# Graph attention's scores as two more columns of the values' product, row vectors turned on VectorE, queries and keys in one tile

## The chip, the cores and the metric

The kernel runs on one core of a Trainium2 chip. The metric is the device time of one execution in microseconds. The core has five engines that run their own instruction streams in order and meet through semaphores: TensorE (PE, matrix products and transposes, which write to the accumulation memory PSUM), VectorE (DVE), ScalarE (ACT), GpSimd (POOL) and SyncE (SP), whose queue issues nearly all of this kernel's DMA transfers.

## The reference

Four graph layers over eight independent batches of 2048 nodes with 128 features, all float32, on one 0/1 adjacency matrix. Before each layer stands a layer norm and a ReLU, and each layer's result is added to its input:

```python
h = maximum(layernorm(x), 0); x = x + layer0(h, adj, W, a, node_weights, ...)
h = maximum(layernorm(x), 0); x = x + layer1(h, adj, W_q, W_k, W_v, W_o, b_o)
h = maximum(layernorm(x), 0); x = x + layer2(h, adj, W_self, W_neigh, ...)
h = maximum(layernorm(x), 0); x = x + layer3(h, adj, W, a)
```

Layers 0 and 3 are graph attention. Their scores come from two dot products of each node's projected features h (layer 0's h is normalised once more, scaled by gamma and shifted by beta):

```python
s1 = h @ a[:128]; s2 = h @ a[128:]                  # two numbers for each node
e = leaky_relu(s1[:, :, None] + s2[:, None, :], 0.2)
att = softmax(where(adj > 0, e, -inf)); out = att @ h
```

Layer 1 is masked attention with four heads of 32. Layer 2 is a mean over the neighbours and two products. Layer 0 ends in an ELU, layer 2 in a ReLU.

## The kernel before, in words

One batch is four chunks g of 512 nodes, each a tile of 128 partitions x 4 x 128 features; nodes are also counted in 16 tiles of 128. At the start, mask_steps reads the adjacency (16 x 1 MB) and writes packed and transposed masks to DRAM, while layer0_ahead(0) prepares the first batch.

The backbone is layer 1's attention, all heads and batches: mains is a list of small steps (12 for each block of 256 rows and one head), which use PE for scores (L876), transposes (L912) and values (L927), DVE for the masked scores with their minimum (L892), and ACT for the exponentials (L900) and the copies of the transposed weights (L917). All other layers are side work. Function work puts the side steps between the main steps so that the weights given by hand are used up evenly over the batch. While batch b is in layer 1, the side does layers 2 and 3 of batch b - 1 and layer 0 of batch b + 1. For the first batch and for layers 2 and 3 of the last there is nothing to put them beside.

The order of instructions on PE, DVE, ACT and POOL is the order in which the code calls them (manual_schedule); the waits between engines are put in by the framework. SP's DMAs follow their places in the code.

A product in PSUM is read late. psum takes one of three buffers of two banks each from pool ps2, and later puts off the reader until the next side step begins (settle) or until buffers run short; the attention holds up to three of them itself.

What the change touches:

- layer0_ahead runs over the chunks in a skewed pipeline of stages: load, first layer norm, weigh (POOL), turned (PE transposes, ACT copy), project (rows_times with w0, ACT copy to haug, L561), second layer norm, scale and shift (POOL, L567 and L570), turned2 (PE transposes of haug, ACT copy h0nT), gat_scores.
- gat_scores (L374) multiplies each transposed tile on PE with the two vectors a (tile psc, L383); DVE copies the columns to s1 and s2 and makes s2n (L386 to L388). Layer 3 does the same with h3T and the vectors W a (wa3).
- along_free (L355) makes a row that all partitions hold from a column over partitions: PE transposes it to PSUM (prow, L360), DVE copies it (row, L364), SP writes it to DRAM (rowd, L366), and a second DMA broadcasts it to all partitions (L367). gat_rows does this with s2n for tile s2b, once for a layer. spread does it for each of the six groups of rows in gat_loop, with s1 and the row maximum in tile cab, for tile ab.
- gat_loop's groups: gat_maximum (L404) takes the maximum of s2 over the neighbours, shifts makes cab, spread sends it, then leaky (ACT, L464), lowered (DVE, L470), exps (ACT, L474), masked (DVE, L479) and product (PE, L490) run over the columns. A group's rows are sent while the group before is in its loop; a layer's first group has only its own ahead steps before it.
- before_attention.project makes queries (pq, L643) and keys (pk, L652) in two PSUM tiles, each with an ACT copy (qs, kc) and a DMA to DRAM.

Of the kernel before, what the change touches and what calls it, by code (L numbers as in the profile page):

```python
# [31 lines left out]
def gnn_kernel(  # L32
# [104 lines left out]
    def chunk(s):  # L137

        return new(cp, "c", s, (P, 512))
# [36 lines left out]
    nc.gpsimd.memset(neg_half, -0.5)  # L176

# [10 lines left out]
    w0 = load_w("w0", W0)  # L188
# [16 lines left out]
    NR = 2 * T + 4  # L205
# [4 lines left out]
    nc.scalar.dma_start(out=rows[2 * T + 2 : NR], in_=a3.rearrange("(c f) o -> c (f o)", c=2))  # L210
# [76 lines left out]
    def norm_stages(src, dst, relu=False):  # L287
# [44 lines left out]

        return [stats, root, shift, apply_relu] if relu else [stats, root, apply]
# [14 lines left out]
    def rows_times(srcT, w, name):  # L348

        pt = psum(name)  # L350
        for k in range(4):
            nc.tensor.matmul(pt[:, k, :], srcT[:, k * P : (k + 1) * P], w, start=True, stop=True)
        return pt

    def along_free(col, dst):  # L355


        n = col.shape[1]
        pt = psum("prow", (n, P))
        nc.tensor.transpose(pt, col, ident)  # L360

        def read():
            row = small("row", (T, P))[0:n, :]
            nc.vector.tensor_copy(row, pt)  # L364
            d = new(dr2, "rowd", "rowd", (T, P))
            nc.sync.dma_start(out=d[0:n, :], in_=row)  # L366
            nc.sync.dma_start(  # L367
                out=dst, in_=d[0:n, :].rearrange("t p -> (t p)").partition_broadcast(P)
            )

        later(read)


    def gat_scores(st, g, hT, a12):  # L374

        if g == 0:
            st["s1"] = small("s1", (P, T))
            st["s2"] = small("s2", (P, T))
            st["s2n"] = small("s2n", (P, T))
        c = slice(4 * g, 4 * g + 4)  # L380
        pc = psum("psc", (P, 4, 2))
        for k in range(4):
            nc.tensor.matmul(pc[:, k, :], hT[:, k * P : (k + 1) * P], a12, start=True, stop=True)  # L383

        def read():
            nc.vector.tensor_copy(st["s1"][:, c], pc[:, :, 0])  # L386
            nc.vector.tensor_copy(st["s2"][:, c], pc[:, :, 1])
# [20 lines left out]
    def gat_loop(st, finish, maxima):  # L408
# [20 lines left out]
        def shifts(k):  # L429
# [4 lines left out]
            cab = small("cab", (P, 6))[:, 0 : 2 * n]  # L434
# [101 lines left out]
    def layer0_ahead(b):  # L536

        st, h, hT, h2T = {}, {}, {}, {}
# [17 lines left out]
        def project(g):  # L556
# [4 lines left out]
            later(lambda: nc.scalar.copy(st["haug"][:, 4 * g : 4 * g + 4, 0:P], pt))  # L561
# [10 lines left out]
        def turned2(g):  # L572
            h2T[g] = chunk("h0nT")
            turn(hv(g), h2T[g])
# [7 lines left out]
            + norm_stages(hv, hv)  # L582
            + [scale, shift, turned2, lambda g: gat_scores(st, g, h2T.pop(g), a12_0)],
# [37 lines left out]
    def before_attention(b):  # L621
# [19 lines left out]
        def project(g):  # L641
            pq = psum("pq", (P, 512))
            nc.tensor.matmul(pq, wq, hT[g], start=True, stop=True)  # L643

            def read_q():
                qs = chunk("qs")
                nc.scalar.activation(qs, pq, AF.Copy, scale=-1.0 / (math.sqrt(HD) * UP))
# [4 lines left out]
            nc.tensor.matmul(pk, wk, hT[g], start=True, stop=True)  # L652

            def read_k():
# [650 lines left out]
```

## Time and profile before

| | |
|---|---|
| median of 3 runs | 4863.75 us (4861.99 to 4867.91) |
| the profiled execution | 4871.3 us, span 4869.5 us |
| PE, DVE, ACT busy | 4236.4, 3863.5, 3643.9 us |
| a steady batch (891 to 1462 us) | 571.0 us |
| granted PE clock, mean | 0.946 |
| DMA | 423.37 MB, mean 87 GB/s |

In the profile a group is a line of the kernel with one shape: how often it ran, its busy time, the mean of one, and the idle time of its engine just before it, with what ended that. PEld is PE's load of weights. The chain of waits follows the execution back from its last instruction, at each step to what released it. A stretch is a piece of the span with the busy time of each engine in it.

### The profile page before, as it was taken

To read this page: it belongs to the slowest core of one execution; us is meant where nothing else is said; L and a number is where in the kernel's file an instruction comes from. 1 tells how busy PE (TensorE), PEld (TensorE's weight loads), DVE (VectorE), ACT (ScalarE), POOL (GpSimd) and SP (SyncE) were. 2 spreads that over 40 slices of the span, in tenths; PEclk is the share of its full clock that TensorE was granted. 3 is DMA by queue.
4 is the path that set the end of the run, shared out by engine and by line. 5 is a ranking of instruction groups with operands and counts; after the bars stand their busy time and mean duration, and the time that the engine had idled before them with its cause. 6 is when DMAs were issued, how large, how long until landed. Compare 5 with 4: busy or idle time off the path is not lost.

```text
span 4869.5 us, 88275 instructions
## 1 busy us (share of the span) xinstructions
PE 4236.4 (87%) x34037; PEld 2898.0 (60%) x34037; DVE 3863.5 (79%) x8268; ACT 3643.9 (75%) x5153; POOL 437.4 (9%) x407
## 2 busy tenths in 40 slices
PE   3668998898998889898898988988899988999976
PEld 3545655565656666475665656566565656656645
DVE  5957776788978888788987889788887888758849
ACT  4637986697858888497885978588884888848926
POOL 2020002001200021001200012000210000000000
PEclk7868999999999999999999999999999999999988
DMA  8421123213231132312333132421324113222122
GB/s 269 135 88 54 47 61 97 92 49 102 81 126 57 57 107 79 124 50 76 91 105 95 57 94 85 122 65 55 107 76 130 48 58 98 79 86 62 47 92 75
DMA packets 303741, 423.37 MB, mean 87 GB/s; under 512 B 55844, under 2 KB 173016, under 8 KB 299224
## 3 DMA queue, kind: packets, MB, share of 16 engines
q1 hardware_dynamic: 301376, 416.84, 28.2%
q8 instruction: 269, 4.41, 0.4%
q14 instruction: 152, 1.25, 0.1%
q10 hardware_dynamic: 1944, 0.87, 0.1%
HBM read 365.77 MB, written 55.98 MB: 87 GB/s over the span
## 4 chain that ended last, share of the span: by engine, by line
PE 40%; DVE 31%; ACT 21%; issue 4%; DMA 4%; SPq 0%; POOL 0%; ACTq 0%; DVEq 0%; POOLq 0%
DVE e L892 9%; PE gacc L490 9%; PE pt L912 9%; ACT eT L917 6%; ACT e L900 6%; PE pagg L737 6%; PE sc L876 5%; DVE dump L404 5%; DVE ge L479 4%; DVE ge L470 4%; PE acc L927 4%; ACT ge L464 4%; ACT ge L474 2%; DVE ln_s L297 1%; DMA ab<-rowd 1%
## 5 line engine op out<-in xcount | busy, mean ns | idle before, releaser
L917 ACT COPY eT<-pt 128x1024 f32<-128x1024 f32 x1024 | 1018.4, 1011 | 666.4 <-PE pt L912 663.2
L892 DVE CUSTOM_DVE_ANT_0 e<-sc,pm 128x1024 f32<-128x1024 f32 x1024 | 1211.3, 1220 | 214.7 <-PE sc L876 205.6
L912 PE MATMUL pt<-ident,e 128*128 128x128 f32 x8192 | 1098.5, 282 | 187.0 <-DVE amh L892 106.0
L490 PE MATMUL gacc<-haug,ge 128*128 128x129 f32 x8192 | 1114.1, 286 | 123.4 <-DVE ge L479 121.2
L490 PEld LDWEIGHTS gacc<-haug,ge 128*128 128x128 f32 x8192 | 1011.9, 198 | 264.4 <-issue 134.7
L912 PEld LDWEIGHTS pt<-ident,e 128*128 128x128 f32 x8192 | 940.2, 145 | 341.4 <-DVE amh L892 137.4
L900 ACT ACTIVATE e<-e,amn 128x2048 f32<-128x2048 f32 x512 | 1027.8, 2007 | 20.9 <-DVE amn L896 20.8
L464 ACT ACTIVATE ge<-ab,s 128x384 f32<-128x384 f32 (+1 forms) x1536 | 800.6, 574 | 96.6 <-DMA ab<-rowd 96.3
L876 PE MATMUL sc<-ks,qr 32*128 32x512 f32 x4096 | 765.2, 668 | 55.8 <-ACT eT L917 40.5
L470 DVE TENSOR_TENSOR ge<-ge,ab 128x768 f32<-128x768 f32 (+1 forms) x768 | 666.4, 869 | 112.5 <-ACT ge L464 107.6
L479 DVE SCALAR_TENSOR_TENSOR ge<-mg,ge 128x768 f32<-128x768 fp8e4 (+1 forms) x768 | 662.0, 863 | 87.3 <-ACT ge L474 85.2
L474 ACT ACTIVATE ge<-ge 128x768 f32<-128x768 f32 (+1 forms) x768 | 591.5, 772 | 78.4 <-DVE ge L470 75.0
L927 PE MATMUL acc<-eT,vv 128*32 128x256 f32 x8192 | 612.5, 400 | 3.9 <-ACT eT L917 3.8
L404 DVE CUSTOM_DVE_ANT_0 dump<-s2b,pmg 128x2048 bf16<-128x2048 f32 x256 | 584.7, 2284 | 28.4 <-DMA s2b<-rowd 23.8
L307 POOL TENSOR_TENSOR ln_r<-ln_ve,neg_half 128x4 f32<-128x4 f32 x160 | 224.9, 1405 | 3872.8 <-DVE ln_ve L301 3781.0
L927 PEld LDWEIGHTS acc<-eT,vv 128*32 128x32 f32 x8192 | 196.6, 111 | 509.1 <-issue 430.2
L876 PEld LDWEIGHTS sc<-ks,qr 32*128 32x128 f32 x4096 | 231.9, 190 | 230.7 <-ACT eT L917 120.5
L737 PE MATMUL pagg<-mt,hm 128*128 128x512 fp8e4 x1536 | 356.7, 381 | 7.9 <-DVE agT L755 7.9
L737 PEld LDWEIGHTS <-hm 128*128 128x128 bf16 x1536 | 147.2, 98 | 182.0 <-issue 30.2
L339 PE MATMUL ptr<-ident,h 128*128 128x128 f32 x512 | 93.1, 308 | 46.1 <-DVE h L314 16.6
L980 DVE TENSOR_TENSOR aoT<-po,rT 128x256 f32<-128x256 f32 x64 | 27.1, 424 | 125.0 <-ACT rT L975 125.0
L339 PEld LDWEIGHTS ptr<-ident,h 128*128 128x128 f32 x512 | 65.5, 154 | 87.2 <-issue 26.6
(120 smaller groups left out, 2779.4 us busy)
## 6 DMA issues: line engine op xcount, KB each, us to landing
pmg<-pm_all SPq DMA_DIRECT2D x256, 256.0 KB
mg<-mg_all SPq DMA_DIRECT2D x128, 384.0 KB
pm<-pm_all SPq DMA_DIRECT2D x128, 256.0 KB
qr<-qd SPq DMA_DIRECT2D x1024, 32.0 KB
mt<-mt_all SPq DMA_DIRECT2D x64, 512.0 KB
ab<-rowd SPq DMA_DIRECT2D x64, 384.0 KB
adj<-in_adj_dram SPq DMA_DIRECT2D x16, 1024.0 KB
s2b<-rowd SPq DMA_DIRECT2D x16, 1024.0 KB
```

Of the source, the lines that this page charges most:

```text
L404: nc.vector.tensor_tensor_reduce(dump, st["s2b"], pm, UP, HIGHEST, ALU.add, ALU.min, st["mn"][:, it : it + 1])
L464: nc.scalar.activation(e[:, c, :], gr[k]["s1"], AF.Prelu, bias=st["s2"][:, j : j + 1], alpha=ALPHA)
L470: nc.vector.tensor_tensor(e, e, bc_mid(gr[k]["m"], 2), ALU.subtract)
L479: nc.vector.scalar_tensor_tensor(e, mt, BIG, e, ALU.mult, ALU.min)
L490: nc.tensor.matmul(gr[k]["acc"][:, q, :], e[:, c, q * P : (q + 1) * P], st["haug"][:, j, :], start=(j == 0 and q == 0), stop=(j == T - 1), ...
L737: nc.tensor.matmul(st["pa"], st["hm"][:, j, s, :], st["mt", g, j // 8][:, j % 8, :], start=(j == 0 and s == 0), stop=(j == T - 1 and s == ...
L876: nc.tensor.matmul(blk["sc"][g // 2][:, (g % 2) * 512 : (g % 2 + 1) * 512], blk["q"][r, t * P : (t + 1) * P], ks_t[b, hh][r, :], start=Tru ...
L892: nc.vector.tensor_tensor_reduce(e[:, c], blk["sc"][h], pm[:, c], UP, HIGHEST, ALU.add, ALU.min, mh[:, h : h + 1])
L900: nc.scalar.activation(blk["e"][t], blk["e"][t], AF.Exp, scale=-1.0, bias=blk["mn"][:, t : t + 1], accum_out=blk["ao"]["sum"][:, t, blk["h ...
L912: nc.tensor.transpose(pt[:, c, t, :], blk["e"][t][:, j * P : (j + 1) * P], ident)
L917: nc.scalar.copy(eT, blk.pop(("pt", w)).rearrange("p c t n -> p c (t n)"))
L927: nc.tensor.matmul(pair["acc"][g * HD : (g + 1) * HD, blk["hh"] % 2, :], vv_t[blk["b"], blk["hh"]][:, j, :], blk["eT"][w][:, g, :], start= ...
```

## The change

The scores of both graph attention layers become two more columns of the product that makes the values. For layer 3, W a is appended to W's transpose (w3T becomes 128 x 130). For layer 0, W (gamma a) is appended to w0; since the norm lies between, DVE corrects the two columns with the mean, the inverse root and two pairs of constants (gab: the sums of gamma a and of beta a). The transposes turned2 and the products psc go. The stage gat_scores of layer 0 stands before the norm is applied, and in layer 3 it is part of the reading of the product.

along_free turns a 128 x 32 tile on DVE in blocks of 32 x 32, and four DMAs, one for each 32 partitions, write the pieces to DRAM; its reading is no longer put off. The tiles cab and s2n become fixed tiles of 32 columns. Queries and keys share one PSUM tile, and both are read after both products. The set-up computes the additional columns.

```diff
--- before.py
+++ after.py
@@ -174,6 +174,15 @@
     )
     neg_half = const.tile([P, T], F32, name="neg_half")
     nc.gpsimd.memset(neg_half, -0.5)
+    cabs = [const.tile([P, 32], F32, name=f"cab{k}") for k in range(3)]
+    s2ns = [const.tile([P, 32], F32, name=f"s2n{k}") for k in range(2)]
+    for t in cabs + s2ns:
+        nc.gpsimd.memset(t, 0.0)
+    turns = {"cab": 0, "s2n": 0}
+
+    def next_of(name, ts):
+        turns[name] += 1
+        return ts[turns[name] % len(ts)]
 
     def load_w(name, ap):
         t = const.tile([P, P], F32, name=name)
@@ -185,7 +194,9 @@
         nc.scalar.dma_start(out=t, in_=ap.partition_broadcast(P))
         return t
 
-    w0 = load_w("w0", W0)
+
+    w0 = const.tile([P, P + 2], F32, name="w0")
+    nc.scalar.dma_start(out=w0[:, 0:P], in_=W0)
     wq = load_w("wq", W_q)
     wk = load_w("wk", W_k)
     wv = load_w("wv", W_v)
...
+    nc.scalar.dma_start(out=rows[2 * T + 4 : 2 * T + 5], in_=ln_g.rearrange("(o f) -> o f", o=1))
+    nc.scalar.dma_start(out=rows[2 * T + 5 : NR], in_=ln_b.rearrange("(o f) -> o f", o=1))
    cols = const.tile([P, NR], F32, name="cols")
     pcol = psum("pcol", (P, NR))
     nc.tensor.transpose(pcol, rows, ident[:NR, :NR])
@@ -216,16 +231,35 @@
     nc.vector.tensor_scalar(nw1, cols[:, 0:T], 1.0, None, ALU.add)
     nb = cols[:, T : 2 * T]
     a12_0 = cols[:, 2 * T : 2 * T + 2]
-    a12_3 = cols[:, 2 * T + 2 : NR]
-    w3T = const.tile([P, P], F32, name="w3T")
+    a12_3 = cols[:, 2 * T + 2 : 2 * T + 4]
+
+
+    ga = const.tile([P, 4], F32, name="ga")
+    for c in range(2):
+        nc.vector.tensor_scalar(
+            ga[:, 2 * c : 2 * c + 2], a12_0, cols[:, 2 * T + 4 + c : 2 * T + 5 + c], None, ALU.mult
+        )
+    ones = const.tile([P, P], F32, name="ones")
+    nc.gpsimd.memset(ones, 1.0)
+    pga = psum("pga", (P, 4))
+    nc.tensor.matmul(pga, ones, ga, start=True, stop=True)
+    gab = const.tile([P, 4], F32, name="gab")
+    nc.vector.tensor_copy(gab, pga)
+    w0T = const.tile([P, P], F32, name="w0T")
+    pw0 = psum("pw0", (P, P))
+    nc.tensor.transpose(pw0, w0[:, 0:P], ident)
+    nc.vector.tensor_copy(w0T, pw0)
+    pwa0 = psum("pwa0", (P, 2))
+    nc.tensor.matmul(pwa0, w0T, ga[:, 0:2], start=True, stop=True)
+    nc.vector.tensor_copy(w0[:, P : P + 2], pwa0)
+    w3T = const.tile([P, P + 2], F32, name="w3T")
     pw3 = psum("pw3", (P, P))
     nc.tensor.transpose(pw3, w3, ident)
-    nc.vector.tensor_copy(w3T, pw3)
-
-    wa3 = const.tile([P, 2], F32, name="wa3")
+    nc.vector.tensor_copy(w3T[:, 0:P], pw3)
+
     pwa = psum("pwa", (P, 2))
     nc.tensor.matmul(pwa, w3, a12_3, start=True, stop=True)
-    nc.vector.tensor_copy(wa3, pwa)
+    nc.vector.tensor_copy(w3T[:, P : P + 2], pwa)
 
     GROUPS = [(0, 3), (3, 3), (6, 3), (9, 3), (12, 2), (14, 2)]
@@ -330,6 +364,7 @@
                     d[:, k, :], t[:, k, :], AF.Relu, bias=m[:, k : k + 1], scale=r[:, k : k + 1]
                 )
 
+        stats.st = st
         return [stats, root, shift, apply_relu] if relu else [stats, root, apply]
 
     def turn(src, dst, func=AF.Copy, to=None):
@@ -347,52 +382,53 @@
 
     def rows_times(srcT, w, name):
 
-        pt = psum(name)
+        n = w.shape[1]
+        pt = psum(name, (P, 4, P if n == P else 2 * P))
         for k in range(4):
-            nc.tensor.matmul(pt[:, k, :], srcT[:, k * P : (k + 1) * P], w, start=True, stop=True)
+            nc.tensor.matmul(pt[:, k, 0:n], srcT[:, k * P : (k + 1) * P], w, start=True, stop=True)
         return pt
 
-    def along_free(col, dst):
-
-
-        n = col.shape[1]
-        pt = psum("prow", (n, P))
-        nc.tensor.transpose(pt, col, ident)
-
-        def read():
-            row = small("row", (T, P))[0:n, :]
-            nc.vector.tensor_copy(row, pt)
-            d = new(dr2, "rowd", "rowd", (T, P))
-            nc.sync.dma_start(out=d[0:n, :], in_=row)
+    def along_free(col, dst, n):
+
+
+        row = small("row", (P, 32))
+        nc.vector.transpose(row, col)
+        d = new(dr2, "rowd", "rowd", (T, P))
+        for g in range(4):
             nc.sync.dma_start(
-                out=dst, in_=d[0:n, :].rearrange("t p -> (t p)").partition_broadcast(P)
+                out=d[0:n, g * 32 : (g + 1) * 32], in_=row[g * 32 : g * 32 + n, :]
             )
-
-        later(read)
-
-
-    def gat_scores(st, g, hT, a12):
+        nc.sync.dma_start(
+            out=dst, in_=d[0:n, :].rearrange("t p -> (t p)").partition_broadcast(P)
+        )
+
+
+    def gat_scores(st, g, src, mean=None, r=None):
 
         if g == 0:
-            st["s1"] = small("s1", (P, T))
-            st["s2"] = small("s2", (P, T))
-            st["s2n"] = small("s2n", (P, T))
-        c = slice(4 * g, 4 * g + 4)
-        pc = psum("psc", (P, 4, 2))
-        for k in range(4):
-            nc.tensor.matmul(pc[:, k, :], hT[:, k * P : (k + 1) * P], a12, start=True, stop=True)
-
-        def read():
-            nc.vector.tensor_copy(st["s1"][:, c], pc[:, :, 0])
-            nc.vector.tensor_copy(st["s2"][:, c], pc[:, :, 1])
-            nc.vector.tensor_scalar(st["s2n"][:, c], st["s2"][:, c], -1.0 / UP, None, ALU.mult)
-
-        later(read)
+            st["s"] = small("s", (P, T, 2))
+            st["s1"], st["s2"] = st["s"][:, :, 0], st["s"][:, :, 1]
+            st["s2n"] = next_of("s2n", s2ns)
+        s = st["s"][:, 4 * g : 4 * g + 4, :]
+        if mean is None:
+            nc.vector.tensor_copy(s, src)
+        else:
+            for c in range(2):
+                nc.vector.scalar_tensor_tensor(
+                    src[:, :, c], mean, gab[:, c : c + 1], src[:, :, c], ALU.mult, ALU.subtract
+                )
+            nc.vector.tensor_tensor(src, src, bc_last(r, 2), ALU.mult)
+            nc.vector.scalar_tensor_tensor(
+                s, src, -1.0, bc_mid(gab[:, 2:4], 4), ALU.mult, ALU.add
+            )
+        nc.vector.tensor_scalar(
+            st["s2n"][:, 4 * g : 4 * g + 4], s[:, :, 1], -1.0 / UP, None, ALU.mult
+        )
 
     def gat_rows(st):
 
         st["s2b"] = new(sp2, "s2b", "s2b", (P, N))
-        along_free(st["s2n"], st["s2b"])
+        along_free(st["s2n"], st["s2b"], T)
 
     def gat_maximum(st, it):
 
@@ -431,7 +467,7 @@
             s1 = st["s1"][:, i0 : i0 + n]
             u = small("gu", (P, 3))[:, 0:n]
             nc.vector.tensor_tensor(u, s1, st["mn"][:, i0 : i0 + n], ALU.subtract)
-            cab = small("cab", (P, 6))[:, 0 : 2 * n]
+            cab = next_of("cab", cabs)
             nc.vector.tensor_copy(cab[:, 0:n], s1)
             nc.vector.scalar_tensor_tensor(cab[:, n : 2 * n], u, ALPHA, u, ALU.mult, ALU.max)
             gr[k]["cab"] = cab
@@ -439,7 +475,7 @@
         def spread(k):
             n = GROUPS[k][1]
             t = new(abp, "ab", "ab", (P, 2 * n * P))
-            along_free(gr[k]["cab"], t)
+            along_free(gr[k]["cab"], t, 2 * n)
             gr[k]["s1"], gr[k]["m"] = t[:, 0 : n * P], t[:, n * P : 2 * n * P]
 
         def ahead(k):
@@ -535,7 +571,7 @@
 
     def layer0_ahead(b):
 
-        st, h, hT, h2T = {}, {}, {}, {}
+        st, h, hT, zs = {}, {}, {}, {}
 
         def load(g):
             h[g] = new(hp3, "h", "h", (P, 4, P))
@@ -558,7 +594,13 @@
                 st["haug"] = new(h0p, "h0", "haug", (P, T, P + 1))
                 nc.gpsimd.memset(st["haug"][:, :, P : P + 1], 1.0)
             pt = rows_times(hT.pop(g), w0, "ph")
-            later(lambda: nc.scalar.copy(st["haug"][:, 4 * g : 4 * g + 4, 0:P], pt))
+
+            def read():
+                nc.scalar.copy(hv(g), pt[:, :, 0:P])
+                zs[g] = small("ln_z", (P, 4, 2))
+                nc.vector.tensor_copy(zs[g], pt[:, :, P : P + 2])
+
+            later(read)
 
         def hv(g):
             return st["haug"][:, 4 * g : 4 * g + 4, 0:P]
@@ -569,9 +611,11 @@
         def shift(g):
             nc.gpsimd.tensor_tensor(hv(g), hv(g), bc_mid(bet, 4), ALU.add)
 
-        def turned2(g):
-            h2T[g] = chunk("h0nT")
-            turn(hv(g), h2T[g])
+        norm2 = norm_stages(hv, hv)
+
+        def score(g):
+            mv, r = norm2[0].st[g]
+            gat_scores(st, g, zs.pop(g), mv[:, :, 0], r)
 
         steps = Steps()
         steps.skewed(
@@ -579,8 +623,10 @@
             [load]
             + norm_stages(lambda g: h[g], lambda g: h[g], relu=True)
             + [weigh, turned, project]
-            + norm_stages(hv, hv)
-            + [scale, shift, turned2, lambda g: gat_scores(st, g, h2T.pop(g), a12_0)],
+            + norm2[:2]
+            + [score]
+            + norm2[2:]
+            + [scale, shift],
             1.0,
         )
         return st, steps
@@ -639,24 +685,19 @@
             nc.gpsimd.tensor_tensor(xb[g], xb[g], bc_mid(bo1, 4), ALU.add)
 
         def project(g):
-            pq = psum("pq", (P, 512))
-            nc.tensor.matmul(pq, wq, hT[g], start=True, stop=True)
-
-            def read_q():
+            pt = psum("pqk", (P, 2, 512))
+            nc.tensor.matmul(pt[:, 0, :], wq, hT[g], start=True, stop=True)
+            nc.tensor.matmul(pt[:, 1, :], wk, hT[g], start=True, stop=True)
+
+            def read():
                 qs = chunk("qs")
-                nc.scalar.activation(qs, pq, AF.Copy, scale=-1.0 / (math.sqrt(HD) * UP))
+                nc.scalar.activation(qs, pt[:, 0, :], AF.Copy, scale=-1.0 / (math.sqrt(HD) * UP))
                 nc.sync.dma_start(out=qd[g], in_=qs)
-
-            later(read_q)
-            pk = psum("pk", (P, 512))
-            nc.tensor.matmul(pk, wk, hT[g], start=True, stop=True)
-
-            def read_k():
                 kc = chunk("kc")
-                nc.scalar.copy(kc, pk)
+                nc.scalar.copy(kc, pt[:, 1, :])
                 nc.sync.dma_start(out=kd[g], in_=kc)
 
-            later(read_k)
+            later(read)
 
         def project_v(g):
             pv = rows_times(hT.pop(g), wv, "pv")
@@ -806,16 +847,22 @@
             if g == 0:
                 st["haug"] = new(bp, "big", "haug", (P, T, P + 1))
                 nc.gpsimd.memset(st["haug"][:, :, P : P + 1], 1.0)
-            pt = rows_times(hT[g], w3T, "ph3")
-            later(lambda: nc.scalar.copy(st["haug"][:, 4 * g : 4 * g + 4, 0:P], pt))
+            pt = rows_times(hT.pop(g), w3T, "ph3")
+
+            def read():
+                nc.scalar.copy(st["haug"][:, 4 * g : 4 * g + 4, 0:P], pt[:, :, 0:P])
+                gat_scores(st, g, pt[:, :, P : P + 2])
+
+            later(read)
 
         pre = Steps()
         pre.skewed(
             G,
             norm_stages(lambda g: xb[g], hdst)
-            + [turned, project, lambda g: gat_scores(st, g, hT.pop(g), wa3)],
+            + [turned, project],
             1.0,
         )
+        pre.add(0.5, settle)
         pre.add(1.0, lambda: gat_rows(st))
 
         def finish(i0, n, acc, rec):
...
```

More of the change, by code (lines that the diff above doesn't have):

```diff
@@ L202, in gnn_kernel @@
     nc.vector.tensor_scalar(bo1, bo1, -1.0, None, ALU.add)
-    NR = 2 * T + 4
+    NR = 2 * T + 6
     rows = const.tile([NR, P], F32, name="rows")
@@ L209, in gnn_kernel @@
     nc.scalar.dma_start(out=rows[2 * T : 2 * T + 2], in_=a0.rearrange("(c f) o -> c (f o)", c=2))
-    nc.scalar.dma_start(out=rows[2 * T + 2 : NR], in_=a3.rearrange("(c f) o -> c (f o)", c=2))
+    nc.scalar.dma_start(
+        out=rows[2 * T + 2 : 2 * T + 4], in_=a3.rearrange("(c f) o -> c (f o)", c=2)
+    )
+    nc.scalar.dma_start(out=rows[2 * T + 4 : 2 * T + 5], in_=ln_g.rearrange("(o f) -> o f", o=1))
+    nc.scalar.dma_start(out=rows[2 * T + 5 : NR], in_=ln_b.rearrange("(o f) -> o f", o=1))
     cols = const.tile([P, NR], F32, name="cols")
@@ L367, in read @@
             nc.sync.dma_start(
[L368 removed]
+                out=d[0:n, g * 32 : (g + 1) * 32], in_=row[g * 32 : g * 32 + n, :]
             )
[L371 to L374 removed]
+        nc.sync.dma_start(
+            out=dst, in_=d[0:n, :].rearrange("t p -> (t p)").partition_broadcast(P)
+        )
+    def gat_scores(st, g, src, mean=None, r=None):
         if g == 0:
[L377 to L390 removed]
+            st["s"] = small("s", (P, T, 2))
[15 more added lines that the diff above has]
+            st["s2n"][:, 4 * g : 4 * g + 4], s[:, :, 1], -1.0 / UP, None, ALU.mult
+        )
@@ L1128, in degrees @@
             nc.tensor.transpose(pt, dinv, ident)
-            row = small("row", (T, P))
+            row = const.tile([T, P], F32, name="dvr")
             nc.vector.tensor_copy(row, pt)
```

## The prediction

> **What bounds the kernel now.** I read the page first, then the stretches by stage, then the groups by form, then the waits, then the chain.
>
> ```profile
> PE 4236.4 (87%) x34037; PEld 2898.0 (60%) x34037; DVE 3863.5 (79%) x8268; ACT 3643.9 (75%) x5153; POOL 437.4 (9%) x407
> ...
> PE 40%; DVE 31%; ACT 21%; issue 4%; DMA 4%; SPq 0%; POOL 0%; ACTq 0%; DVEq 0%; POOLq 0%
> ```
>
> PE is the fullest engine, but the chain that ends last spends only 40% of the span on it: three engines hand the path to each other. Work taken from PE is worth less than its own length, and work put on DVE costs about a third of it.
>
> The stretches, one steady batch of them:
>
> ```profile
> core 0: us, PE busy (x) PEld busy (x) DVE busy (x) ACT busy (x) POOL busy (x), PEclk, DMA share, GB/s
> ...
> 891.00:1462.00 571.00, 517.76 (x4222) 353.87 (x4222) 475.85 (x1029) 448.08 (x639) 59.18 (x50) 0.97 0.28 86
> ```
>
> In a batch of 571 us PE is busy 518, DVE 476, ACT 448. DMA moves 86 GB/s at a share of 0.28, so bandwidth bounds nothing there; latency can.
>
> The costliest groups that the change takes away:
>
> ```profile
> L383 PE MATMUL psc<-cols,h0nT 128*128 128x2 f32 x256 | 37.4, 268 | 6.6 <-ACT h0nT L342 6.5
> ...
> L383 PE MATMUL psc<-wa,h3T 128*128 128x2 f32 x256 | 33.9, 254 | 0.2 <-ACT haug L810 0.2
> ...
> L339 PE MATMUL ptr<-ident,haug 128*128 128x128 f32 x128 | 23.4, 313 | 5.3 <-DVE s L387 2.8 <-POOL haug L570 1.0 <-DVE x L990 0.6
> ...
> L386 DVE COPY s<-psc 128x4 f32<-128x4 f32 x64 | 10.1, 158 | 90.5 <-PE psc L383 90.4
> ```
>
> A product of two columns (psc, 268 ns) costs PE almost as much as one of 128. DVE stands idle 90 us for it. In the same list stand the ACT copies h0nT (32 of 595 ns), PE's prow transposes (112, about 0.29 us) and the DVE copies of them (112 of 272 ns).
>
> Waits that matter for what is added:
>
> ```profile
> ACT haug L810 <- PE ph L352: 31.4, 20, 4.5
> ...
> DVE ln_s L297 <- ACT haug L561: 18.4, 11, 4.5
> ...
> PE pk L652 <- ACT qs L647: 12.6, 5, 2.5
> ```
>
> And the chain at the first group of a layer's loop, where a row vector is late:
>
> ```profile
> 905.57 0.28 PE prow L360
> 905.86 0.03 issue
> 905.88 0.29 DVE row L364
> 906.17 0.02 issue
> 906.19 1.48 DMA rowd<-row
> ...
> 907.73 4.33 DMA ab<-rowd
> ```
>
> The hop over PE and PSUM takes 0.6 us; the write to DRAM and the broadcast after it take ten times that.
>
> **The change part by part.** The sums on the path below add up the chain's pieces by name over the whole profiled execution (span 4869.5 us, 4871.3 with what lies around it; the median of the runs shown is 4863.75, 7.55 less).
>
> *Scores in the values' product.* Gone: 64 psc tiles (8 matmuls, about 0.95 us each tile at full clock: 4722.93 to 4723.88 in the timeline, and 1.9 us in the start), 32 tiles of four haug transposes (0.63 us), 32 ACT copies h0nT. On the chain this is psc 45.6 us; ptr 44.6 us over 640 transposes, of which 128 go, a fifth, 8.9; h0nT 4.5; the copies L386 and L387 6.1. Together 65. Not all of it comes back: where PE's piece is taken out of a mixed stretch, DVE or ACT, busy 83% and 78% there, is late next. In the start, the second and third batch's preparation and the last layer there is little beside it. I count three quarters: -49. The two columns more in 512 matmuls I cost at nothing: the 129-column products of L490 take 275 ns, like the 128-column ones.
>
> *DVE's new work.* Layer 0 had three small instructions for each chunk of four tiles and gets six (one copy of the columns, four for mean, inverse root and constants, one for s2n); layer 3 goes from three to two. Rows of L386 to L388 start 0.08 us apart where independent and 0.18 where one needs the other; the new four are mostly a chain, so some 0.9 us against 0.3: 32 x 0.6 = 19 us more on DVE, 31% of it on the path: +6. Layer 3's 32 x 0.1 saved is in the rounding.
>
> *A new wait.* The columns sit in the tile ph that ACT copies to haug. In the trace, one layer-3 step: ph done at 990.14, DVE at its score copy at 990.61, ACT's haug copy from 990.82 to 991.38. If DVE may read the tile while ACT does, it waits for nothing here. The page "PSUM — Partial Sum Buffer" of the Trainium skill, section on PSUM bank collisions, says that two engines must not access one bank in the same partitions at once, two reads included, and that such pairs are therefore put in order. No run here shows this case. By the rule DVE waits until 991.38, 0.77 us; by the row alone, none. I go by the rule, since ACT's copy comes first in the code: 32 x 0.77 in layer 3, and in layer 0, where the statistics already wait for that copy (the 18.4 us above), 32 x 0.5: 41 us idle, a third on the path: +13 (none to +52, see the rival). Behind the waiting copy on DVE stand the attention's masked scores L892, and PE's transposes wait for these.
>
> *Row vectors on DVE.* 112 PE transposes and 112 copies of 272 ns go; 112 block transposes of 128x32 come. The trace has none; bounded by the small copies (0.15) and by the row copy (0.27), I take 0.16, as 32 elements a partition are nearer to the former. On the chain prow and row stand for 15.8 us; the transposes give 6 back: -10. Against that, one DMA of up to 16 rows becomes four, 336 more on SP's queue. The four queries of L861 take 1.73 us to issue, 0.43 each, so the broadcast is issued 1.3 us later. The write is on the chain 16 times: +21. Where the row is fetched two or more loop steps ahead, the extra 1.3 us is hidden by those steps; without that cover all 112 would cost 146 us. The rows written are also 128 B instead of 512. The page "DMA: Bandwidth & Descriptors", Specifications, calls for 512 B or more and says smaller ones are read, modified and written. Here a write of 512 B rows takes 1.16 to 1.5 us until the broadcast is issued; one more trip to memory, which that page (Latency) gives as 0.2 us on average and 2 us under load, makes 16 x 0.2 = 3 to 32 us. I take 0.2, since the DMA share is 0.28, and leave it inside the rounding of the 21. The DMAs are also issued a loop step earlier, as nothing is put off until PSUM is read: past queries (L861), masks (L421) and mask rows (L402) that SP would have issued before. Those have a block or a step of slack; SP waited 483 us at L366 for the row in any case.
>
> *Queries and keys in one tile.* PE no longer waits for ACT qs before pk (12.6 us on PE, 16.7 on its weight loads), and one buffer fewer turns over; but the queries' copy now starts after both products, 1.2 us later, and kc behind it. Both go to DRAM for the next batch, so this is hidden. On the path: -5 (0 to -15).
>
> *Set-up.* Two more row DMAs on ACT's queue, three small PE groups, seven small DVE instructions, six POOL memsets. DVE idles 5.2 us for the adjacency at 26 us and hides 3 us of it; ACT's first mask comes 1 to 2 us later: +2 (0 to +5).
>
> Sum: -49 + 6 + 13 - 10 + 21 - 5 + 2 = -22 us. On the profiled execution 4849, on the median 4842.
>
> **The rivals.**
>
> *PE is the bound after all.* Then all of PE's removed time counts: 71 + 23 + 33 us busy = 127, less the 35 or so added elsewhere, about -90: 4774. For it: 518 of 571 us. Against it: 40% of the chain, and DVE at 83% beside it.
>
> *Hidden anyway.* Other engines are late at once and only a third of the 65 comes back: -22 instead of -49, total +5: 4869, no difference. For it: the chain changes engine some thousand times; the waits of DVE for psc become waits for ph, which PE reaches no sooner.
>
> *DVE waits for a busy ACT.* The columns' copy is queued behind ACT's whole backlog: one exponential L900 of 2.0 us and the copy of 0.59 make 2.6 us. 64 x 2.6 = 166 us idle, 31% of it 52 instead of 13: total +17, 4881, and more in the stretches where DVE has most of the path. It decides from the point where the mean wait passes 0.64 + 22/(64 x 0.31), about 1.75 us. For it: ACT is busy 78% and in order, and DVE is often first at such reads. Against it: in 20 of 32 cases of layer 3 it was ACT that waited for PE, so its copy starts at once.
>
> That the change doesn't do what it says has little room: every removed group has its own line.
>
> **How the numbers follow.** The likeliest case (-22, from -10 to -45) has 0.44; PE as the bound (-45 to -125) 0.14; hidden (within 10 us) 0.17; slower through the wait, the DMAs, or both 0.25. About 0.2% (10 us) is what a measurement of this kernel can tell from no change. So faster by more than that 0.58, within it 0.17, slower 0.25. The range is 4780 to 4885: below lies the far end of the second case, above the worse half of the fourth. The likeliest case alone is 4818 to 4854.
>
> **What would show it.** Right: L383, haug transposes and prow gone, PE busy some 125 us less, DVE's busy time within 15 us of before; a steady batch of about 568 us; the wait of DVE for psc replaced by a smaller one at the columns' copy, on ACT haug; rowd to broadcast about 2.5 us on the chain. Wrong: the columns' copy waits 2 us or more each time, or the ab broadcasts become a wait of ACT well above the 96 us of now, or the batch shortens by ten us or more, which would make PE the bound.

## The result and the profile after

The changed kernel takes 4888.79 us (median of 5 runs, 4885.07 to 4889.26); the kernel before, on the same chip, 4867.91. The ratio is 1.0041, 95% interval 1.0027 to 1.0056: slower by some 20 us. The prediction said 4842 and faster, with a range that ended at 4885. Both sign and size were wrong.

The page of the kernel after, its line of engines and its line of the chain:

```profile
PE 4162.5 (85%) x33290; PEld 2828.6 (58%) x33290; DVE 3892.2 (80%) x8337; ACT 3619.5 (74%) x5121; POOL 433.4 (9%) x413
...
PE 36%; ACT 29%; DVE 27%; issue 4%; DMA 3%; SPq 1%; ACTq 0%; DVEq 0%
```

Beside the page of before, PE has 74 us less to do, DVE 29 more, ACT 24 less. And yet the path moved to ACT, from 21% to 29%: an engine with less work carries more of the path.

The steady batch that the prediction showed (571 us), between the same two attention steps:

```profile
887.00:1465.00 578.00, 508.67 (x4135) 344.46 (x4133) 482.00 (x1037) 446.83 (x636) 58.64 (x50) 0.96 0.28 85
```

PE's busy time fell by 9 us and the batch grew, by 5 us if it is taken from one attention exponential to the same one a batch later (571.0 to 576.4; the window shown is a little wider). The work did go; what grew is idle time.

The groups that took the place of psc, haug's transposes and prow (busy us, mean ns, then the idle time before them and its releaser):

```profile
L388 PE MATMUL ph<-w,h0T 128*128 128x130 f32 x256 | 39.7, 303 | 18.4 <-DVE amh L939 8.7 <-ACT h0T L377 8.6 <-DVE aoT L1027 1.0
L424 DVE TENSOR_SCALAR s2n<-s 128x4 f32<-128x4 f32 x64 | 24.0, 374 | 2.2
L417 DVE SCALAR_TENSOR_TENSOR ln_z<-ln_mv,gab,ln_z 128x4 f32<-128x4 f32 x64 | 20.2, 358 | 0.0
L395 DVE STREAM_TRANSPOSE row<-cab 128x32 f32<-128x32 f32 x96 | 19.7, 205 | 0.5
L420 DVE TENSOR_TENSOR ln_z<-ln_z,ln_r 128x8 f32<-128x8 f32 x32 | 19.4, 606 | 3.3
...
L421 DVE SCALAR_TENSOR_TENSOR s<-ln_z,gab 128x8 f32<-128x8 f32 x32 | 5.3, 167 | 1.3 <-DVE ln_z L420 0.2
...
L601 DVE COPY ln_z<-ph 128x8 f32<-128x8 f32 x32 | 5.3, 165 | 45.1 <-ACT haug L599 44.7
L414 DVE COPY s<-ph 128x8 f32<-128x8 f32 x32 | 5.2, 163 | 46.7 <-ACT haug L853 46.6
```

Two things stand out. The two copies of the columns are short, and DVE is idle 91.8 us before them. And a product of eight elements a partition (L420) takes 606 ns on average, where its neighbour L421, of the same size, takes 167.

The waits of DVE at the columns (us, times, longest):

```profile
DVE s L414 <- ACT haug L853: 46.6, 18, 3.6
DVE ln_z L601 <- ACT haug L599: 44.7, 20, 4.4
```

These 91.3 us stand where 90.4 us of waiting for psc stood before: one wait took the other's place. One instance is seen in the timeline of the kernel after, in one step of layer 0's preparation (start, duration):

```profile
1821.25 1.16 PE L388 MATMUL ph<-w,h0T 128*128 128x130 f32 x8
1821.95 1.12 ACT L500 ACTIVATE ge<-ab,s 128x384 f32<-128x384 f32 x2
1822.96 0.58 ACT L599 COPY haug<-ph 128x512 f32<-128x512 f32 x1
...
1823.58 0.17 DVE L601 COPY ln_z<-ph 128x8 f32<-128x8 f32 x1 [4.05 <-ACT haug L599]
1823.66 1.21 DVE L939 CUSTOM_DVE_ANT_0 e<-sc,pm 128x1024 f32<-128x1024 f32 x1
1823.89 0.63 PE L374 MATMUL ptr<-ident,h 128*128 128x128 f32 x4 [1.48 <-DVE ln_z L601]
```

PE is done with the tile at 1822.41. ACT reaches its copy at 1822.96, after the loop's two L500, and ends at 1823.54; DVE, idle for 4.05 us, copies at 1823.58. So ACT, which the view names because it came last, accounts for 1.17 of the 4.05 us; for the other 2.88 the product itself was not there. Taken over all 38 of these waits in the trace, the 91.3 us are 54 until PE's product is done, 14 until ACT begins its copy, and 23 for that copy: 37 us come through ACT. Behind the copy of the columns stands the attention's masked minimum L939, whose scores PE had finished at 1820.3. Then PE waits for DVE.

### The profile page after: what moved, and what is told of

It reads as the page before. It is cut to its first block, busy times and chain, and to the rows that moved or that the text cites. A ratio compares the mean times of both kernels' runs of the same rounds, so it can differ in the third digit from the quotient of the medians.

```text
span 4886.4 us, 87216 instructions
## 1 busy us (share of the span) xinstructions
PE 4162.5 (85%) x33290; PEld 2828.6 (58%) x33290; DVE 3892.2 (80%) x8337; ACT 3619.5 (74%) x5121; POOL 433.4 (9%) x413
## 4 chain that ended last, share of the span: by engine, by line
PE 36%; ACT 29%; DVE 27%; issue 4%; DMA 3%; SPq 1%; ACTq 0%; DVEq 0%
PE pt L959 9%; ACT e L947 8%; ACT eT L964 8%; PE gacc L526 8%; DVE e L939 7%; PE pagg L778 6%; ACT ge L500 6%; DVE dump L440 5%; PE sc L923 5%; PE acc L974 4%; ACT ge L510 4%; DVE ge L515 3%; DVE ge L506 3%; DVE ln_s L331 1%; DMA ab<-rowd 1%
## 5 line engine op out<-in xcount | busy, mean ns | idle before, releaser
L939 DVE CUSTOM_DVE_ANT_0 e<-sc,pm 128x1024 f32<-128x1024 f32 x1024 | 1210.4, 1219 | 196.9 <-PE sc L923 179.7
L959 PE MATMUL pt<-ident,e 128*128 128x128 f32 x8192 | 1113.3, 284 | 228.8 <-DVE amh L939 103.2
L526 PE MATMUL gacc<-haug,ge 128*128 128x129 f32 x8192 | 1128.2, 289 | 170.7 <-DVE ge L515 162.7
L500 ACT ACTIVATE ge<-ab,s 128x384 f32<-128x384 f32 (+1 forms) x1536 | 801.7, 576 | 90.4 <-DMA ab<-rowd 90.0
```

What stands on the lines that cost most here:

```text
L500: nc.scalar.activation(e[:, c, :], gr[k]["s1"], AF.Prelu, bias=st["s2"][:, j : j + 1], alpha=ALPHA)
L526: nc.tensor.matmul(gr[k]["acc"][:, q, :], e[:, c, q * P : (q + 1) * P], st["haug"][:, j, :], start=(j == 0 and q == 0), stop=(j == T - 1), ...
L939: nc.vector.tensor_tensor_reduce(e[:, c], blk["sc"][h], pm[:, c], UP, HIGHEST, ALU.add, ALU.min, mh[:, h : h + 1])
L959: nc.tensor.transpose(pt[:, c, t, :], blk["e"][t][:, j * P : (j + 1) * P], ident)
```

## The experiments

Each ratio is against runs of the kernel before on the same chip; "x us" below is the ratio's difference from 1 times 4865.

**The parts one by one.** Four kernels, each the kernel before with one part of the change.

Row vectors on VectorE, alone:

```diff
-        pt = psum("prow", (n, P))
-        nc.tensor.transpose(pt, col, ident)
...
+        row = small("row", (P, 32))
+        nc.vector.transpose(row, col)
+        d = new(dr2, "rowd", "rowd", (T, P))
+        for g in range(4):
             nc.sync.dma_start(
...
+                out=d[0:n, g * 32 : (g + 1) * 32], in_=row[g * 32 : g * 32 + n, :]
             )
...
```

> The kernel before with one part of the change alone: row vectors turned by DVE block transposes and written by four DMAs; scores, queries and keys as before. Theory A (the loss lies in layer 0's preparation: DVE's new score arithmetic and its wait for ACT's copy): this part costs or gives little, 4855 to 4875. Rival B (the three extra DMAs make the row vectors late): slower by 15 to 35 us, with ACT's wait for the ab rows well above 96 us and the broadcast some 1.3 us later after the row. The prediction's own term for this part was -10 + 21 = +11.

4845.94 us, ratio 0.9963 (0.9951 to 0.9975): 18 us faster. The late row vectors of rival B are not there: ACT's wait for the ab rows is 100.7 us, 96.3 before.

Queries and keys in one tile, alone:

```diff
-            pq = psum("pq", (P, 512))
...
+            pt = psum("pqk", (P, 2, 512))
...
-            pk = psum("pk", (P, 512))
...
```

> The kernel before with queries and keys in one two-bank tile, nothing else. Theory A: PE no longer waits 12.6 us for the queries' copy, -2 to -8 us. Rival C (the later copies and the two-bank tile hold a buffer longer and stop PE elsewhere): slower by 5 to 15 us, with new waits of the turned h1T tiles for ACT kc. The prediction's term was -5.

4848.31 us, ratio 0.9966 (0.9953 to 0.9978): 17 us faster, twice the most that was expected.

Layer 0's scores as two more columns, alone (w0 of 130 columns, the stages h0nT and scores out, one score stage in):

```diff
-            + norm_stages(hv, hv)
-            + [scale, shift, turned2, lambda g: gat_scores(st, g, h2T.pop(g), a12_0)],
+            + norm2[:2]
+            + [score]
+            + norm2[2:]
+            + [scale, shift],
```

> The kernel before with the scores of layer 0 alone as two more columns (one step fewer in the preparation); layer 3, row vectors, queries and keys as before. Theory A: this part carries the loss, +15 to +30 us, all of it in the stretches in which the next batch's layer 0 is prepared: small DVE instructions of the score stage take 0.97 instead of 0.17 us where POOL works beside them, and DVE's copy of the columns waits about 2 us for ACT's copy. Rival B (rows): this part gains 10 to 25 us. Rival D (it is only that other main steps stand beside the preparation's steps): a loss, but not at these instructions.

4955.59 us, ratio 1.0185 (1.0171 to 1.0199): 90 us slower, three times what theory A allowed, and not where it said. Counted from one attention exponential to the next, a steady batch of some 590 us (570 before) loses 4 to 5 us already in the stretch of layer 2, where no instruction of layer 0's preparation stands. Something other than the new instructions costs time. What else differs is the number of steps: 17 where there were 18.

Layer 3's scores alone:

```diff
-            later(lambda: nc.scalar.copy(st["haug"][:, 4 * g : 4 * g + 4, 0:P], pt))
+            def read():
+                nc.scalar.copy(st["haug"][:, 4 * g : 4 * g + 4, 0:P], pt[:, :, 0:P])
+                gat_scores(st, g, pt[:, :, P : P + 2])
```

> The kernel before with the scores of layer 3 alone as two more columns; layer 0, row vectors, queries and keys as before. Theory A: a gain of 8 to 20 us, most of it at the end of the kernel, where nothing lies beside the last layer's preparation; DVE's wait of about 2.5 us for ACT's copy takes some of it back in the steady batches. Theory E (the wait for ACT's copy is the whole cause): this part loses too, 5 to 15 us, as both copies wait alike (46.6 and 44.7 us in the changed kernel).

4860.42 us, ratio 0.9985 (0.9977 to 0.9993): 7 us faster, just short of theory A.

**The steps' weights.** The side work is spread over the attention's steps by weights, and each step of this preparation weighs 0.5: 17 steps weigh 8.5, 18 weigh 9. So the weights alone were changed, in the kernel before:

```diff
         )
+        steps[:] = [(w * 17 / 18, f) for w, f in steps]
         return st, steps
```

> The kernel before, every instruction the same; only the weights of the 18 steps of layer 0's preparation are multiplied by 17/18, so that they sum to 8.5, as the 17 steps of the change do, and all side work of a batch shifts a little against the attention's steps. Theory D (the loss is mostly that other main steps stand beside the side work): 15 us slower or more. Theory A (the new score arithmetic and its waits cost the time): within 8 us of before.

4949.45 us, ratio 1.0173 (1.0159 to 1.0187): 84 us slower without one instruction changed. One steady batch of the kernel before, and the batch between the same attention steps of this one:

```profile
1338.00:1908.00 570.00, 514.59 (x4231) 351.00 (x4223) 476.39 (x1028) 448.30 (x640) 59.16 (x50) 0.97 0.29 86
...
1355.00:1944.00 589.00, 522.76 (x4226) 358.15 (x4222) 477.46 (x1027) 447.97 (x639) 64.74 (x50) 0.95 0.28 83
```

DVE and ACT are as busy as before, PE 8 us longer, at a granted clock of 0.95 in place of 0.97; the batch takes 19 us more. So the clock's part, in so far as PE's busy time shows it, is at most 8 of the 19; the rest is waiting. A stretch of its timeline shows what a shifted step does:

```profile
1840.42 1.63 ACT L329 ACTIVATE h<-h,ln_m,ln_r 128x128 f32<-128x128 f32 x4
1840.76 1.83 PE L877 MATMUL sc<-ks,qr 32*128 32x512 f32 x8
1842.66 1.22 DVE L893 CUSTOM_DVE_ANT_0 e<-sc,pm 128x1024 f32<-128x1024 f32 x1 [1.96 <-PE sc L877]
...
1848.47 1.64 ACT L329 ACTIVATE h<-h,ln_m,ln_r 128x128 f32<-128x128 f32 x4
1851.06 1.61 PE L877 MATMUL sc<-ks,qr 32*128 32x512 f32 x8 [0.91 <-ACT eT L918]
...
1852.23 1.23 DVE L893 CUSTOM_DVE_ANT_0 e<-sc,pm 128x1024 f32<-128x1024 f32 x1 [2.67 <-PE sc L877]
```

Two of ACT's four-part activations of the preparation (L329) fall between two of the attention's exponentials, where the kernel before has one. The second stands on ACT shortly ahead of the copy eT that PE's scores wait for, and DVE is idle for 1.96 and 2.67 us; in the kernel before it reaches both masked minima of this step without a wait. From one exponential to the next it is 15.8 us here, 12.5 there.

With weights of 19/18 in the same place:

> The kernel before, every instruction the same, with the weights of layer 0's preparation multiplied by 19/18, so that the side work shifts the other way. If the old placing is only one of many (a shift either way changes the time by chance): 4850 to 4900, or even faster. If the weights of before stand at a narrow best: 4900 to 4960, like the shift by 17/18.

4876.34 us, ratio 1.0021 (1.0013 to 1.0029): 10 us slower. A shift either way costs, in very unequal amounts. Of these three placings that of before is the best.

**The changed parts at the step counts of before.** An empty stage at the end of a preparation gives it back its steps and its functions:

```diff
-            + [scale, shift],
+            + [scale, shift, lambda g: None],
```

For layer 0's scores alone:

> Layer 0's scores as two more columns, as in the part alone that was 88 us slower, with one empty stage more in its preparation: 18 steps and as many functions as before, so the side work lies against the attention's steps as before. Theory D: at least half of the 88 us is gone, 4870 to 4910. Theory A: 4940 to 4960, as the score instructions and waits are all still there.

4887.52 us, ratio 1.0047 (1.0034 to 1.006): 23 us slower instead of 90: most of the loss was the step count. Layer 0's scores alone, with DVE copying the columns, still lose time. For the whole change, in both layers (in layer 3 in place of the settling step):

> The changed kernel with an empty stage in layer 0's preparation and one in layer 3's (in place of the settling step), so that both have as many steps and functions as before. Theory D: the change's parts then give what they give one by one, 4820 to 4850. Theory A: 4875 to 4895, as changed.

4857.49 us, ratio 0.9988 (0.998 to 0.9995): 6 us faster than before, 26 us away from the change as it is. And with layer 0's empty stage alone:

> The changed kernel with the empty stage in layer 0's preparation alone (18 steps there, layer 3's preparation as in the change). If the 31 us of both empty stages come from layer 0's count, as the scaled weights of the kernel before say: 4850 to 4865. If from layer 3's: 4880 to 4895.

4858.82 us, ratio 0.9987 (0.998 to 0.9993). So layer 0's count is what costs the 26 us; layer 3's costs nothing measurable. Theory D holds, though it is not the whole story: it also expected 4820 to 4850 here, so that 7 to 37 us are lost elsewhere (the next experiments).

**The columns' copy.** ACT, which has the tile in hand, copies the columns too:

```diff
-            nc.vector.tensor_copy(s, src)
+            nc.scalar.copy(s, src)
+            nc.scalar.activation(
+                st["s2n"][:, 4 * g : 4 * g + 4], src[:, :, 1], AF.Copy, scale=-1.0 / UP
+            )
...
-                nc.vector.tensor_copy(zs[g], pt[:, :, P : P + 2])
+                nc.scalar.copy(zs[g], pt[:, :, P : P + 2])
```

The first part is layer 3's, where ACT also makes s2n; the last is layer 0's.

First on the change with its own step counts:

> The changed kernel with its own steps, but ACT copies the two columns after its copy of the other 128 (in layer 3 also the negated second column), so DVE waits for no copy of ACT at these places. Theory E (DVE's wait of 91 us for ACT's copies is the cause): 20 to 40 us faster than the changed kernel, 4850 to 4870. Theories A (arithmetic) and D (other neighbours): 5 us faster to 5 us slower than the changed kernel; ACT gains some 25 us of busy time in 96 small copies.

4868.18 us, ratio 1.0005 (0.9997 to 1.0014): 18 us faster than the change. Then at the step counts of before:

> The changed kernel with the step counts of before (an empty stage in each preparation) and with ACT copying the two columns, so DVE waits for none of ACT's copies there. If DVE's wait costs the path some 20 us wherever the side work lies: 4832 to 4842. If the 20 us that ACT's copies brought at the other step counts were luck of the neighbours: 4850 to 4862.

4789.70 us, ratio 0.9845 (0.9831 to 0.9859): 75 us faster than the kernel before, 70 faster than the same kernel with the copies on DVE. No forecast above reached that far. The wait that went is larger there than in the change, as the waits of DVE in the kernel with empty stages say:

```profile
DVE s L414 <- ACT haug L853: 69.4, 23, 4.8
...
DVE ln_z L601 <- ACT haug L599: 63.6, 27, 9.5
```

Split as before, these 133 us are 61 until PE's product is done, 42 until ACT begins its copy and 30 for the copy. So 72 us come through ACT, twice the 37 of the change, and the time is 70 us shorter without them. The three small copies cost ACT 0.17 to 0.19 us each. The chain's line of this kernel:

```profile
PE 37%; DVE 33%; ACT 22%; issue 5%; DMA 3%; SPq 1%; ACTq 0%; DVEq 0%
```

ACT is back at 22%, though it has 96 more instructions: it is waited for less. The clock may have a part in the 70 us: PE's busy time, of the same products, is 4165.3 us with DVE's copies (granted clock 0.936) and 4130.6 with ACT's (0.942). These 35 us are at most half of the gain.

Is it the wait or the copy on DVE? In the next kernel, again at the step counts of before, DVE keeps the copies and makes them first:

> The changed kernel with the step counts of before, and the order of the two reads turned: DVE copies the two columns first and ACT copies the 128 after it. DVE keeps every instruction and waits for PE alone. If DVE's wait for ACT is what cost 68 us there: 4785 to 4805, with ACT waiting a little for DVE's columns in its place. If the copy on DVE itself cost it, or if the wait only changes sides: 4835 to 4860.

4828.15 us, ratio 0.9929 (0.9915 to 0.9942): 29 us better than with ACT first, 41 us short of ACT alone. It lies between the two forecasts, and its waits say why:

```profile
DVE ln_z L600 <- PE ph L388: 39.0, 20, 8.9
DVE s L414 <- PE ph L388: 36.3, 14, 3.2
ACT haug L854 <- DVE s L414: 23.3, 14, 5.0
ACT haug L601 <- DVE ln_z L600: 20.3, 16, 2.4
```

DVE still stands idle for 75 us, now for PE, and ACT 44 us for DVE. The 75 us of waiting for the product stay, as the split above would have it, and the waiting between ACT and DVE changed sides in part. The reading that fits is that the copy costs less by its own 0.17 us than because a third engine must meet the other two at this tile; no run here takes these two apart.

**Beside POOL.** L420's instances take either 0.17 or about 1 us, and each of the 17 long ones runs while POOL scales haug (L609; once it shifts it, L612): POOL's scaling starts when DVE's apply ends, and DVE's next work is the score stage. The score stage was put behind the apply stage, at the step counts of before:

```diff
-            + [score]
-            + norm2[2:]
-            + [scale, shift],
+            + [applied, score]
+            + [scale, shift, lambda g: None],
```

> The changed kernel with the step counts of before, and in layer 0's preparation the score stage one place later, after the stage that applies the norm: POOL's scaling then no longer starts together with the score instructions on DVE. If the blocking by POOL costs the path its third: the small score instructions fall back to 0.17 us from 0.97, some 30 us of DVE time, and the time to 4842 to 4850. If DVE time there is beside other work: 4855 to 4860 with the same short instructions.

4851.81 us, ratio 0.9971 (0.9959 to 0.9982). The groups of this kernel:

```profile
L424 DVE TENSOR_SCALAR s2n<-s 128x4 f32<-128x4 f32 x64 | 12.6, 197 | 2.2
L420 DVE TENSOR_TENSOR ln_z<-ln_z,ln_r 128x8 f32<-128x8 f32 x32 | 8.1, 253 | 1.1
```

The collision is mostly gone: 20.7 us for the two where the kernel with empty stages has 48.1 (24.8 and 23.3). The time is 8 us less by the ratios, but the intervals overlap, so that this gain is not shown.

Both edits together:

> Both edits together on the changed kernel with the step counts of before. If the wait and the blocking are separate costs: 4820 to 4835. If one hides the other: as the better of the two.

4786.72 us, ratio 0.9835 (0.9821 to 0.9848): the best kernel here, 100 us faster than the change by the two ratios. The order of the stages adds 5 us by the ratios, which again is within the error.

**Rows, queries and keys without the scores.**

> The kernel before with the two parts that gained alone (row vectors on DVE; queries and keys in one tile) and the scores as before. If the gains add: 4865 - 22 - 16 = 4825 to 4835. If they are the same gain (a PE that waits less at one place): 4842 to 4850.

4828.16 us, ratio 0.9919 (0.9905 to 0.9932): 39 us faster than before. The two gains add up (18 + 17 = 35, within the error).

## Why the prediction was wrong

The step that failed is one that the prediction put at nothing without a reason: that a stage less in layer 0's preparation moves all side work of a batch against the attention. Together with the wait at the columns' copy, whose price depends on that placing, it costs 96 us where the sum had 13.

The experiments can be put in one line, from the kernel before to the change: rows, queries and keys -39 (forecast +6); scores in the values' product, with ACT copying the columns, another -36 (0.9919 to 0.9845; forecast -41); DVE copying them instead +70 (forecast +13); the step counts of the change +26 (forecast nothing). Together some +20, the measured result. The last two depend on each other: taken in the other order, with ACT's copies the step counts cost 78 us (1.0005 against 0.9845), and with the step counts of the change DVE's copies cost 18, not 70. Only their sum, 96, is free of the order. That the sum of the prediction is off by no more than 42 us is luck: rows, queries and keys came out 45 us better than forecast, and hid half of the 83 us that these two were short.

- *Scores in the values' product* (-49) with the new arithmetic (+6) and the set-up (+2): as a sum near, -36 against -41, at the old step counts. The three were not measured apart. On the chain, psc went from about 45 us to none and ptr from about 45 to 35. The two further columns are free, as assumed: the median product of 130 columns takes 275 ns, like that of 128 before. The arithmetic is under-counted: the six groups L414, L417, L420, L421, L424 and L601 take 79 us, L386 to L388 took 33, so that DVE has 47 us more and not 16, in part because POOL stretches them. Shortening two of these groups by 27 us brought no gain that is clear of the error.
- *A new wait* (+13, none to +52): the mechanism is the one that was named. DVE's copy starts 0.04 us after ACT's ends, as the page "PSUM — Partial Sum Buffer" of the Trainium skill (section on PSUM bank collisions) let expect of a pair that is put in order. For the change as it stands the size is right too: 37 us come through ACT where 41 were forecast, and 18 us of time where 13 were. At the old step counts it fails, by the idle time (72) and by the share on the path, nearly all of it instead of a third. The estimate came from steps of the kernel before; how far ACT is behind at this tile depends on the placing of the side work, 14 us in all in the change and 42 at the old counts.
- *Rows on DVE* (-10 + 21): +11 forecast, -18 measured. The transposes took 205 ns, not 160, and still the chain's hop fell by the 10 us forecast (prow and row 15.8, row now 5.9). The failed term is the 21. The chain of the kernel after, at the place shown before:

```profile
902.01 0.13 DVE cab L472
...
902.16 0.22 DVE row L395
...
902.40 0.26 SPq L398
...
903.38 1.16 DMA rowd<-row
...
904.56 3.24 DMA ab<-rowd
```

From the end of cab to the broadcast it is 2.42 us; it was 2.29. Three more issues do cost about 1 us, but the way from cab to the first issue (0.75 to 0.25) and the write (1.48 to 1.16) give most of it back. The price of 128 B rows shows nowhere: the nine writes on the chain of the kernel after take 1.15 to 1.45 us each, the sixteen of before 1.15 to 2.57. What the prediction also left out are PE's own waits at prow, 40.8 us idle in the groups of before (26.2, 8.4 and 6.2), mostly for DVE's cab: with the transposes off PE's queue these went too. That they make up the gain is argued, not shown.
- *Queries and keys in one tile* (-5, at most -15): -17. Sign right, size three times; why it is so much is open.
- *Nothing at all* for the number of steps: the step that is missing. The prediction followed each instruction, its queue and its waits, but not that one stage less changes the weights by which all side work of a batch is placed. It costs 26 us in the change, 78 with ACT's copies, and the same shift alone costs 84 in the kernel before. Without it the change would have been faster, if only by 6 us. That the placing is the cause is shown; why this placing is worse by so much is seen in one step only.

Without the wait and at the step counts of before, the sum of the prediction would be -35; measured are -75. The difference of 40 is the 45 of rows, queries and keys, less 5 of the scores.

Of the rivals, "DVE waits for a busy ACT" names a wait that exists, but gives ACT's backlog too much: it put 2.6 us on each of the 64 copies, where in the change 37 us come through ACT in all. It put the decision at a mean wait of 1.75 us. The change has 91.3/64 = 1.43, below that, and was slower all the same, for the step counts. At the old counts the mean is 2.1 us and the price 70 us, more than the 52 that the rival allowed. "PE is the bound" is excluded for the change as it stands: PE lost 74 us of work and the time rose. "Hidden anyway" does not hold at the old counts, where the scores with ACT's copies bring 36 us.

Of the signs that were named ahead, one spoke plainly: the columns' copy waits 2.4 us where it waits (91.3/38), though the larger part of that is the wait for the product. Another was missed: DVE's busy time moved by 29 us and not by 15 at most. PE's busy time fell by 74 us and not 125. Part of that goes with the granted clock, 0.946 before and 0.937 after: in the kernel with scaled weights the same two clocks lie 35 us of PE's busy time apart, with no instruction changed.

## What to carry to other kernels

Where work is interleaved by weights, a stage that is added or removed moves everything else: restore the count with an empty stage before judging an edit, and measure the bare shift. When two engines read one tile, the reader that is already there should take the small extra piece with it; a separate copy of 0.17 us on another engine's queue waits here until the first one's copy is done, with all later work of its own engine behind it.

## What was not expected of the hardware

- Small DVE instructions stretch from 0.17 to about 1 us while POOL scales or shifts haug: L420's median is 970 ns in the change, and 606 on average. The Trainium skill's page "SBUF — State Buffer", section "Who interferes with whom", says that a DVE instruction with two SBUF inputs contends with a GpSimd instruction that reads SBUF, over a pair of ports that they share. The trace fits: L420 reads both inputs from SBUF, and 16 of its 17 long instances start 0.2 us after POOL's scaling, which takes 1.18 us, and end with it.
- A DVE block transpose of 128x32 takes 205 ns.
- With no instruction changed, PE's busy time rose from 4236.4 to 4271.7 us in the kernel with scaled weights, at a granted clock of 0.937 instead of 0.946. Busy time is thus no fixed sum of work. How much of the 84 us comes by the clock, and how much by the waits, stays open; by PE's busy time the clock's part is at most 35.
